# Layer 1: the norm over channels taken with the tokens still on the partitions

## The chip, the cores and the metric

The kernel runs on one core of a Trainium2 chip. Times are microseconds (us) of device time for one execution. Five engines work side by side, each through its own list of instructions in order: TensorE (PE in the profile: matmuls, and PEld for the loading of the stationary operand), VectorE (DVE), ScalarE (ACT), GpSimd (POOL) and SyncE (SP), which issues the DMA transfers. They wait for each other through semaphores. Data lies in SBUF, 128 partitions wide; matmuls write to PSUM[...], and VectorE or ScalarE must copy ("evict") results out of it. The clock that is granted to TensorE (PEclk) varies between half and full.

## The reference

A stack of four layers works on 4 images of 96 channels and 64 x 64 positions, so 16,384 tokens of 96 channels. Layer 0 is a state-space model, layer 2 linear attention and a quantised MLP, layer 3 a Fourier mixer and a second quantised MLP. The change is in layer 1, which computes, for every token:

```
h = conv7x7_depthwise(x) + conv_b
mu, var over the 96 channels
h = (h - mu) * rsqrt(var + 1e-5) * ln_g + ln_b
h = gelu(h @ w1 + b1)          # 96 -> 384, exact gelu
h = h @ w2 + b2                # 384 -> 96
x = h * layer_scale + x
```

## The kernel before

All is float32 in layer 1. `layer1` has two halves. In the first, the output of layer 0 is finished (`tokens`), put in `t` with the channels on the partitions ([96, 16384], the residual), and transposed on TensorE (`turn`) into `xt`, which has 128 neighbouring positions (two image rows) on the partitions and, in the free dimension, channel, image and row pair: `xt[128, 96, 4, 36]`. The convolution is done channel by channel as a matmul with banded 128 x 128 matrices: four matmuls per channel into one slice of a PSUM tile (four buffers) `ps[128, 4 channels, 4 images, 32 row pairs]`. A loop over 24 groups of four channels loads the bands, multiplies, and evicts the whole PSUM tile back into `xt` in one copy of 128 x 512: even groups on ScalarE (L779), odd ones on VectorE (L777). The convolution's bias isn't added there; it is carried, less its mean, in a [96, 1] vector `cb` that a small matmul makes (L740, L741).

The second half is the norm and the MLP, in 32 blocks of 512 tokens (four groups of 128). It needs the channels on the partitions. Per block:

- `back` (L786 to L791): four matmuls with the identity transpose four slices `xt[:, :, b, 2 + r + d]` to `ps[96, 512]`; the slice is the stationary operand, 96 columns that lie 4 x 36 floats, that is 576 bytes, apart. VectorE copies the result to `acc`.
- `centered` (L794 to L799): a matmul with `center` (identity minus 1/96) takes off the mean over channels; ScalarE squares the result with the bias `cb` added, VectorE copies it with `cb` added to `xc`.
- `normed` (L802 to L807): a matmul with a 96 x 96 matrix of ones sums the squares over channels, in every row; ScalarE takes Ln and then Exp of -0.5 times it (the reciprocal root), and GpSimd multiplies `xc` by it.
- `hidden` (L810 to L815): three matmuls to 384 hidden channels, each evicted by ScalarE with Gelu.
- `out` (L818 to L823): three matmuls back to 96 channels, added to the residual `t` by VectorE.

Gelu and Ln/Exp need different tables on ScalarE, so blocks go in rounds of four: all four `normed` of a round (with the `back` of the next round between them), then `hidden` and `out` of the four, with the `centered` of the next round between them. The order on TensorE, VectorE, ScalarE and GpSimd is that of the program text (`manual_schedule`): an engine that waits holds up all that is behind it. A tile's `bufs` says how many buffers it rotates through. PSUM of this half before: one bank for `tp_ps`, two for `xc_ps` and `v_ps` together, four for `g_ps`, one for `m_ps`.

Of the kernel before, what the change touches and what calls it, by code (L numbers as in the profile page):

```python
# [9 lines left out]
F32 = mybir.dt.float32  # L10
# [3 lines left out]
AF = mybir.ActivationFunctionType  # L14
ALU = mybir.AluOpType
# [3 lines left out]
B, C, HW, L = 4, 96, 64, 4096  # L19
NT = B * L  # L20
T = 1024
NSC = L // T
MB = 512
# [4 lines left out]
ACT_EXP_LN = "natural_log_exp_and_others"  # L28
# [22 lines left out]
class Net:  # L51
# [643 lines left out]
    def layer1(self, scratch, t):  # L695
        tc, nc, ins = self.tc, self.nc, self.ins
        NR = L // 128
        GC = 4
        engines = {mybir.EngineType.PE, mybir.EngineType.DVE, mybir.EngineType.Activation, mybir.EngineType.Pool}
        with ExitStack() as ctx:  # L700
            xpool = ctx.enter_context(tc.tile_pool(name="l1x", bufs=1))
            xt = xpool.tile([128, C, B, NR + 4], F32, name="xt")
            cb = xpool.tile([C, 1], F32, name="cb")
            with (
                tc.manual_schedule(engines=engines),
                tc.tile_pool(name="l1a", bufs=1) as wk,
# [28 lines left out]
                for k, chunk in enumerate(chunks):  # L735
                    if k + 1 < len(chunks):
                        tokens(*chunks[k + 1])
                    turn(*chunk)
                ps = psum.tile([128, 4, C], F32, name="cb_ps", tag="xt", bufs=4)[:C, 0, :1]
                nc.tensor.matmul(ps, self.center, self.v("c_b"), start=True, stop=True)  # L740
                nc.vector.tensor_copy(cb, ps)  # L741

                def load(g):
                    w = wk.tile([128, GC, 4, 128], F32, name="band", tag="band", bufs=3)
                    nc.sync.dma_start(w, ins["band"][g])
                    return w
# [14 lines left out]
                for g in range(C // GC):  # L761
                    if g == 8:
                        self.consts2(wk, small)
                    if g % 2 == 0 and g + 2 < C // GC:
                        x2.append(outer(g // 2 + 1))
                    w = load(g)
                    ps = psum.tile([128, GC, B, NR], F32, name="cv_ps", tag="cv", bufs=4)
                    for d in range(GC):
                        c = g * GC + d
                        for k, j in enumerate((1, 0, 2)):  # L770
                            nc.tensor.matmul(
                                ps[:, d], w[:, d, j], xt[:, c, :, 1 + j : 1 + j + NR], start=k == 0, stop=False
                            )
                        nc.tensor.matmul(ps[:, d], w[:, d, 3], x2[g // 2][:, g % 2 * GC + d], start=False, stop=True)
                    dst = xt[:, g * GC : (g + 1) * GC, :, 2 : 2 + NR]
                    if g % 2:
                        nc.vector.tensor_copy(dst, ps)  # L777
                    else:
                        nc.scalar.copy(dst, ps)  # L779

            wk = ctx.enter_context(tc.tile_pool(name="l1w", bufs=1))
            psum = ctx.enter_context(tc.tile_pool(name="l1p", bufs=1, space=PSUM))
            acc, sq, xc, g = {}, {}, {}, {}

            def back(i):
                ps = psum.tile([C, 4, 128], F32, name="tp_ps", tag="tp")  # L786
                b, r = divmod(4 * i, NR)
                for d in range(4):
                    nc.tensor.matmul(ps[:, d], xt[:, :, b, 2 + r + d], self.ident, start=True, stop=True)
                acc[i] = wk.tile([C, MB], F32, name="acc", tag="acc", bufs=5)  # L790
                nc.vector.tensor_copy(acc[i], ps.rearrange("p r n -> p (r n)"))  # L791

            def centered(i):
                ps = psum.tile([C, MB], F32, name="xc_ps", tag="ln", bufs=2)  # L794
                nc.tensor.matmul(ps, self.center, acc.pop(i), start=True, stop=True)
                sq[i] = wk.tile([C, MB], F32, name="sq", tag="sq", bufs=6)
                nc.scalar.activation(sq[i], ps, AF.Square, bias=cb)
                xc[i] = wk.tile([C, MB], F32, name="xc", tag="xc", bufs=9)
                nc.vector.tensor_scalar_add(xc[i], ps, cb)  # L799

            def normed(i):
                ps = psum.tile([C, MB], F32, name="v_ps", tag="ln", bufs=2)  # L802
                nc.tensor.matmul(ps, self.ones, sq.pop(i), start=True, stop=True)
                rs = wk.tile([C, MB], F32, name="rs", tag="rs", bufs=3)
                nc.scalar.activation(rs, ps, AF.Ln, scale=1.0 / C, bias=self.eps[:C])
                nc.scalar.activation(rs, rs, AF.Exp, scale=-0.5)  # L806
                nc.gpsimd.tensor_mul(xc[i], xc[i], rs)  # L807

            def hidden(i):
                g[i] = wk.tile([128, 3, MB], F32, name="g", tag="g", bufs=3)  # L810
                n = xc.pop(i)
                for m in range(3):
                    ps = psum.tile([128, MB], F32, name="g_ps", tag="g", bufs=4)
                    nc.tensor.matmul(ps, self.c_w1[:, m * 128 : (m + 1) * 128], n, start=True, stop=True)
                    nc.scalar.activation(g[i][:, m, :], ps, AF.Gelu, bias=self.c_b1[:, m : m + 1])  # L815

            def out(i):
                ps = psum.tile([C, MB], F32, name="m_ps", tag="m")  # L818
                for m in range(3):
                    nc.tensor.matmul(ps, self.c_w2[:, m, :], g[i][:, m, :], start=m == 0, stop=m == 2)  # L820
                g.pop(i)
                td = t[:, i * MB : (i + 1) * MB]
                nc.vector.scalar_tensor_tensor(td, ps, self.c_b2, td, ALU.add, ALU.add)  # L823


            n = NT // MB
            with tc.manual_schedule(engines=engines):
                for i in range(4):
                    back(i)
                    if i:  # L830
                        centered(i - 1)
                centered(3)
                for i in range(0, n, 4):
                    nc.scalar.preload_act_table_set(ACT_EXP_LN)
                    more = i + 4 < n
                    for d in range(4):
                        normed(i + d)
                        if more:
                            back(i + 4 + d)
                    hidden(i)  # L840
                    for d in range(4):
                        if more:
                            centered(i + 4 + d)
                        if d < 3:
                            hidden(i + d + 1)
                        out(i + d)

    def norm_steps(self, t, wk, psum):

# [499 lines left out]
def _lay_out(i):  # L1349
    f = {k: np.asarray(v) for k, v in i.items()}  # L1350
    m = {k[8:]: v for k, v in f.items() if k.startswith("L0_conv_")}
    c = {k[8:]: v for k, v in f.items() if k.startswith("L1_conv_")}
# [17 lines left out]
    for k, v in (("rd", np.diagonal(a["r"])), ("id", np.diagonal(a["i"])), ("rb", a["rb"]), ("ib", a["ib"])):  # L1370
# [22 lines left out]
        "c_w1": c["w1"],  # L1393
        "c_w2": c["w2"].reshape(3, 128, C).transpose(1, 0, 2),
        "ls_row": c["layer_scale"].reshape(1, C),
        "wkv": aug[:, C:],
        "wqt": aug[:, :C].T,
        "wff": f["L2_attn_Wff"],
# [28 lines left out]
```

## Time and profile before

The time is 4103.03 us, the median of three runs (4100.42 to 4106.08). The profiled execution spans 4106.5 us. Layer 1 in it:

| stretch | us | what it is |
|---|---|---|
| 2612 to 2676 | 64 | `tokens` and `turn` |
| 2676 to 2794 | 118 | convolution, with the loading of constants for later layers between groups 7 and 8 |
| 2794 to 3068 | 274 | norm and MLP, 32 blocks in eight rounds |

The costliest instructions of the last stretch on engines other than TensorE: Gelu 687 ns (three per block), Square 682, Ln 681 and Exp 630 on ScalarE; the copies L791 687, L799 747 and the residual add L823 747 on VectorE; the product L807 1265 on GpSimd; and 16 loads of ScalarE tables of 1283 each, two in a round.

A profile line gives start or line number, engine, operation, output<-input by the program's names, shapes and count. Durations of matmuls are modelled and overlap with those of the next ones, so their sum isn't time; the distance between starts is. A float32 matmul shows as two passes, each with its own LDWEIGHTS.

### The profile page before, as it was taken

How to read it: one execution, taken by the hardware profiler on the slowest of the kernel's cores; microseconds unless marked ns; L12 is line 12 of the kernel's file. 1: busy time of each engine (PE TensorE's matmuls, PEld its weight loads, DVE VectorE, ACT ScalarE, POOL GpSimd, SP SyncE). 2: the span in 40 equal slices, each digit the busy share in tenths (PEclk: the TensorE clock that was granted, in tenths of full speed). 3: DMA queues.
4: the chain of work that ended last, by engine and by line, in shares of the span. 5: the costliest groups of instructions: out<-in, count | busy, mean ns of one | idle time of the engine just before them, and what ended most of it. 6: DMA issues, size and time to landing. Idle time of an engine off the chain costs nothing. (4 is left out here: it accounts for less than half of the span.)

```text
span 4106.5 us, 45550 instructions
## 1 busy us (share of the span) xinstructions
PE 3374.3 (82%) x14304; PEld 1459.6 (36%) x14304; DVE 3125.3 (76%) x2382; ACT 2474.1 (60%) x4690; POOL 2988.3 (73%) x1603
## 2 busy tenths in 40 slices
PE   6788878888888888888777786779999888788987
PEld 3222222222222222222222221575446346555642
DVE  4999999999999999999999999512222673443649
ACT  4676666676667667667666664404555575544547
POOL 2999999999999999999999999321120355333528
PEclk9888878888888888888888886589999998989989
DMA  7567657566666756756656665561000000100111
GB/s 179 142 159 169 148 144 174 138 162 167 154 154 162 166 141 162 175 135 161 171 141 161 168 153 140 146 209 43 0 0 1 0 6 1 29 26 27 47 42 54
DMA packets 183146, 468.08 MB, mean 114 GB/s; under 512 B 53092, under 2 KB 55022, under 8 KB 179824
## 3 DMA queue, kind: packets, MB, share of 16 engines
q1 hardware_dynamic: 182904, 465.17, 45.6%
q8 instruction: 114, 1.87, 0.2%
q14 instruction: 128, 1.05, 0.1%
HBM read 391.48 MB, written 73.50 MB: 113 GB/s over the span
## 5 line engine op out<-in xcount | busy, mean ns | idle before, releaser
L484 POOL TENSOR_TENSOR hs<-hs,crep 128x1024 f32<-128x1024 f32 x768 | 1795.3, 2360 | 28.7 <-DVE hs L478 22.9
L442 PE MATMUL rep<-dbl,sel_b 32*128 32x512 f32 x1152 | 405.4, 780 | 465.7 <-DVE hs L478 439.4
L462 POOL TENSOR_TENSOR up<-udb,brep 128x1024 f32<-128x1024 f32 x256 | 603.9, 2359 | 7.9 <-DMA ud<-du 7.9
L456 ACT ACTIVATE da<-ddb,nega 128x1024 f32<-128x1024 f32 x512 | 584.9, 1149 | 9.7 <-DVE hs L478 8.4
L456 ACT ACTIVATE dap<-ddb,nega 128x1024 f32<-128x1024 f32 x256 | 286.2, 1118 | 418.5 <-DVE hs L478 417.0
L503 PE MATMUL y<-hs,sel_r 128*32 128x512 f32 x3072 | 475.1, 682 | 6.2 <-POOL hs L484 6.1
L478 DVE TENSOR_TENSOR_SCAN hs<-da,state,rep 128x1024 f32<-128x1024 f32 x192 | 450.8, 2348 | 16.7
L478 DVE TENSOR_TENSOR_SCAN hs<-da,state,u 128x1024 f32<-128x1024 f32 x192 | 450.9, 2348 | 10.1
L478 DVE TENSOR_TENSOR_SCAN hs<-dap,state,up 128x1024 f32<-128x1024 f32 x192 | 447.0, 2328 | 5.7 <-ACT dap L456 5.5
L442 PEld LDWEIGHTS rep<-dbl,sel_b 32*128 32x128 f32 x1152 | 108.7, 217 | 758.9 <-issue 513.7
L198 PE MATMUL ps<-n,w_x 97*64 97x512 f32 x1536 | 366.3, 620 | 4.4 <-POOL n L307 4.2
L474 DVE TENSOR_TENSOR u<-udb,rep 128x1024 f32<-128x1024 f32 x256 | 314.7, 1229 | 65.3 <-PE rep L442 43.9
L474 DVE TENSOR_TENSOR rep<-udb,rep 128x1024 f32<-128x1024 f32 x256 | 310.7, 1214 | 0.4
L1013 POOL CAST hq<-y 128x512 fp8e5<-128x512 f16 x192 | 117.9, 638 | 222.0 <-DVE y L1012 221.5
L1161 POOL TENSOR_TENSOR av<-av,ec 128x780 f32<-128x780 f32 x32 | 58.8, 1836 | 195.2 <-ACT av L1158 195.2
L198 PEld LDWEIGHTS ps<-n,w_x 97*64 97x64 f32 x1536 | 108.2, 140 | 253.4 <-issue 202.4
L503 PEld LDWEIGHTS y<-hs,sel_r 128*32 128x32 f32 x3072 | 66.4, 115 | 352.7 <-issue 190.7
L807 POOL TENSOR_TENSOR xc<-xc,rs 96x512 f32<-96x512 f32 x32 | 40.4, 1265 | 208.1 <-ACT rs L806 198.3
L370 POOL TENSOR_TENSOR du<-delta,xc 128x512 f32<-128x512 f32 x96 | 122.0, 1271 | 70.2 <-ACT delta L354 60.6
L212 PE MATMUL ps<-xc,xproj 64*102 64x512 f32 x384 | 155.1, 968 | 3.5 <-ACT xc L332 3.5
L346 ACT COPY dbl<-ps 102x512 f32<-102x512 f32 x64 | 34.3, 588 | 199.7 <-PE ps L212 199.7
L478 DVE TENSOR_TENSOR_SCAN hs<-da,rep 128x1024 f32<-128x1024 f32 x64 | 146.5, 2289 | 5.4
(261 smaller groups left out, 6673.4 us busy)
## 6 DMA issues: line engine op xcount, KB each, us to landing
ddb<-dd SPq DMA_DIRECT2D x768, 128.0 KB, 3.6
udb<-ud SPq DMA_DIRECT2D x768, 128.0 KB, 4.4
crep<-cd SPq DMA_DIRECT2D x512, 128.0 KB, 3.8
brep<-cd SPq DMA_DIRECT2D x256, 128.0 KB, 3.7
dd<-delta SPq DMA_DIRECT2D x64, 384.0 KB, 4.3
ud<-du SPq DMA_DIRECT2D x192, 128.0 KB, 2.5
band<-in_band SPq DMA_DIRECT2D x24, 1024.0 KB, 5.5
gt<-in_idft SPq DMA_DIRECT2D x64, 256.0 KB, 2.7
```

The source lines that it names most:

```text
L198: nc.tensor.matmul(ps[rows], w[:, 64 * p : 64 * p + 64], rhs[:, at.start + shift : at.stop + shift], start=k == 0, stop=k == len(ws) - 1, ...
L212: nc.tensor.matmul(ps, w[rows, p], x[rows, p], start=start and p == 0, stop=p == 2)
L370: nc.gpsimd.tensor_mul(u, m["delta"][:, of], m["xc"][:, of])
L442: nc.tensor.matmul(x[:, at], sel_b[rows, order[t][1]], made[k]["dbl"][rows, at], start=True, stop=True)
L456: nc.scalar.activation(da, made[k]["dd", h, j], AF.Exp, scale=nega[:, col : col + 1])
L462: nc.gpsimd.tensor_mul(u, made[k]["ud", h, j], made[k]["brep", g])
L474: nc.vector.tensor_mul(u, made[k]["ud", h, j], x)
L478: nc.vector.tensor_tensor_scan(hs[:, 1:], made[k].pop(("da", t)), u, 0.0 if s == 0 else st, ALU.mult, ALU.add)
L484: nc.gpsimd.tensor_mul(hs[:, :T], hs[:, 1:], made[k]["crep", order[t][1]])
L503: nc.tensor.matmul(made[k]["y", p][row : row + 32], sel_r, made[k]["hs", t][:, at], start=False, stop=True, skip_group_check=True,)
L1013: nc.gpsimd.tensor_copy(q[:, m, :], y2, saturate=False)
L1161: nc.gpsimd.tensor_add(v[:, 2:4], v[:, 0:2], ec)
```

## The change

The norm is computed before the transposition back, while the 128 partitions of `xt` are tokens and the 96 channels lie in the free dimension. Then mean and variance are sums along the free dimension, which VectorE has instructions for (BN_STATS makes partial statistics of a row, BN_AGGR mean and variance of them), and subtracting the mean and multiplying with the reciprocal root is one TENSOR_SCALAR with two values per partition. What is transposed afterwards is the normed token, in a contiguous tile `n`. The matmuls with `center` and `ones` and the product on GpSimd fall away, and Ln and Exp work on 16 values per partition for a whole round of 2048 tokens. For this the convolution's bias must be in `xt`: it is added in the evictions of the convolution, by channel, from a row that is loaded to all partitions. Statistics and roots are made two rounds ahead of their use (the first two rounds ahead of everything), the transposed blocks one round ahead. The freed PSUM banks double `tp_ps` and `m_ps`.

```diff
@@ -700,7 +700,8 @@
         with ExitStack() as ctx:
             xpool = ctx.enter_context(tc.tile_pool(name="l1x", bufs=1))
             xt = xpool.tile([128, C, B, NR + 4], F32, name="xt")
-            cb = xpool.tile([C, 1], F32, name="cb")
+            cb = xpool.tile([128, C], F32, name="cb")
+            nc.sync.dma_start(cb, ins["c_b_row"].partition_broadcast(128))
             with (
                 tc.manual_schedule(engines=engines),
                 tc.tile_pool(name="l1a", bufs=1) as wk,
@@ -736,9 +737,6 @@
                     if k + 1 < len(chunks):
                         tokens(*chunks[k + 1])
                     turn(*chunk)
-                ps = psum.tile([128, 4, C], F32, name="cb_ps", tag="xt", bufs=4)[:C, 0, :1]
-                nc.tensor.matmul(ps, self.center, self.v("c_b"), start=True, stop=True)
-                nc.vector.tensor_copy(cb, ps)
 
                 def load(g):
                     w = wk.tile([128, GC, 4, 128], F32, name="band", tag="band", bufs=3)
@@ -772,39 +770,47 @@
                                 ps[:, d], w[:, d, j], xt[:, c, :, 1 + j : 1 + j + NR], start=k == 0, stop=False
                             )
                         nc.tensor.matmul(ps[:, d], w[:, d, 3], x2[g // 2][:, g % 2 * GC + d], start=False, stop=True)
-                    dst = xt[:, g * GC : (g + 1) * GC, :, 2 : 2 + NR]
-                    if g % 2:
-                        nc.vector.tensor_copy(dst, ps)
-                    else:
-                        nc.scalar.copy(dst, ps)
+                    for d in range(GC):
+                        c = g * GC + d
+                        dst = xt[:, c, :, 2 : 2 + NR]
+                        if g % 2:
+                            nc.vector.tensor_scalar_add(dst, ps[:, d], cb[:, c : c + 1])
+                        else:
+                            nc.scalar.activation(dst, ps[:, d], AF.Identity, bias=cb[:, c : c + 1])
 
             wk = ctx.enter_context(tc.tile_pool(name="l1w", bufs=1))
             psum = ctx.enter_context(tc.tile_pool(name="l1p", bufs=1, space=PSUM))
-            acc, sq, xc, g = {}, {}, {}, {}
+            mv, rs, xc, g = {}, {}, {}, {}
+
+
+            def stats(k, d):
+                if d == 0:
+                    mv[k] = wk.tile([128, 16, 2], F32, name="mv", tag="mv", bufs=3)
+                for q in range(4 * d, 4 * d + 4):
+                    b, r = divmod(16 * k + q, NR)
+                    st = wk.tile([128, 6], F32, name="st", tag="st", bufs=4)
+                    nc.vector.bn_stats(st, xt[:, :, b, 2 + r])
+                    nc.vector.bn_aggr(mv[k][:, q], st)
+
+            def roots(k):
+                rs[k] = wk.tile([128, 16], F32, name="rs", tag="rs", bufs=3)
+                nc.scalar.activation(rs[k], mv[k][:, :, 1], AF.Ln, bias=self.eps)
+                nc.scalar.activation(rs[k], rs[k], AF.Exp, scale=-0.5)
 
             def back(i):
-                ps = psum.tile([C, 4, 128], F32, name="tp_ps", tag="tp")
-                b, r = divmod(4 * i, NR)
-                for d in range(4):
-                    nc.tensor.matmul(ps[:, d], xt[:, :, b, 2 + r + d], self.ident, start=True, stop=True)
-                acc[i] = wk.tile([C, MB], F32, name="acc", tag="acc", bufs=5)
-                nc.vector.tensor_copy(acc[i], ps.rearrange("p r n -> p (r n)"))
-
-            def centered(i):
-                ps = psum.tile([C, MB], F32, name="xc_ps", tag="ln", bufs=2)
-                nc.tensor.matmul(ps, self.center, acc.pop(i), start=True, stop=True)
-                sq[i] = wk.tile([C, MB], F32, name="sq", tag="sq", bufs=6)
-                nc.scalar.activation(sq[i], ps, AF.Square, bias=cb)
-                xc[i] = wk.tile([C, MB], F32, name="xc", tag="xc", bufs=9)
-                nc.vector.tensor_scalar_add(xc[i], ps, cb)
-
-            def normed(i):
-                ps = psum.tile([C, MB], F32, name="v_ps", tag="ln", bufs=2)
-                nc.tensor.matmul(ps, self.ones, sq.pop(i), start=True, stop=True)
-                rs = wk.tile([C, MB], F32, name="rs", tag="rs", bufs=3)
-                nc.scalar.activation(rs, ps, AF.Ln, scale=1.0 / C, bias=self.eps[:C])
-                nc.scalar.activation(rs, rs, AF.Exp, scale=-0.5)
-                nc.gpsimd.tensor_mul(xc[i], xc[i], rs)
+                k, d = divmod(i, 4)
+                n = wk.tile([128, 4, C], F32, name="n", tag="n", bufs=3)
+                for q in range(4):
+                    b, r = divmod(4 * i + q, NR)
+                    at = slice(4 * d + q, 4 * d + q + 1)
+                    nc.vector.tensor_scalar(
+                        n[:, q], xt[:, :, b, 2 + r], mv[k][:, at, 0], rs[k][:, at], ALU.subtract, ALU.mult
+                    )
+                ps = psum.tile([C, 4, 128], F32, name="tp_ps", tag="tp", bufs=2)
+                for q in range(4):
+                    nc.tensor.matmul(ps[:, q], n[:, q], self.ident, start=True, stop=True)
+                xc[i] = wk.tile([C, MB], F32, name="xc", tag="xc", bufs=7)
+                nc.vector.tensor_copy(xc[i], ps.rearrange("p r n -> p (r n)"))
 
             def hidden(i):
                 g[i] = wk.tile([128, 3, MB], F32, name="g", tag="g", bufs=3)
@@ -815,7 +821,7 @@
                     nc.scalar.activation(g[i][:, m, :], ps, AF.Gelu, bias=self.c_b1[:, m : m + 1])
 
             def out(i):
-                ps = psum.tile([C, MB], F32, name="m_ps", tag="m")
+                ps = psum.tile([C, MB], F32, name="m_ps", tag="m", bufs=2)
                 for m in range(3):
                     nc.tensor.matmul(ps, self.c_w2[:, m, :], g[i][:, m, :], start=m == 0, stop=m == 2)
                 g.pop(i)
@@ -823,27 +829,28 @@
                 nc.vector.scalar_tensor_tensor(td, ps, self.c_b2, td, ALU.add, ALU.add)
 
 
-            n = NT // MB
+            n = NT // MB // 4
             with tc.manual_schedule(engines=engines):
-                for i in range(4):
-                    back(i)
-                    if i:
-                        centered(i - 1)
-                centered(3)
-                for i in range(0, n, 4):
-                    nc.scalar.preload_act_table_set(ACT_EXP_LN)
-                    more = i + 4 < n
+                nc.scalar.preload_act_table_set(ACT_EXP_LN)
+                for k in range(2):
                     for d in range(4):
-                        normed(i + d)
-                        if more:
-                            back(i + 4 + d)
-                    hidden(i)
+                        stats(k, d)
+                    roots(k)
+                for d in range(4):
+                    back(d)
+                for k in range(n):
                     for d in range(4):
-                        if more:
-                            centered(i + 4 + d)
-                        if d < 3:
-                            hidden(i + d + 1)
-                        out(i + d)
+                        hidden(4 * k + d)
+                        if k + 1 < n:
+                            back(4 * k + 4 + d)
+                        if k + 2 < n:
+                            stats(k + 2, d)
+                        if d:
+                            out(4 * k + d - 1)
+                    if k + 2 < n:
+                        nc.scalar.preload_act_table_set(ACT_EXP_LN)
+                        roots(k + 2)
+                    out(4 * k + 3)
 
     def norm_steps(self, t, wk, psum):
 
@@ -1393,6 +1400,7 @@
         "c_w1": c["w1"],
         "c_w2": c["w2"].reshape(3, 128, C).transpose(1, 0, 2),
         "ls_row": c["layer_scale"].reshape(1, C),
+        "c_b_row": c["conv_b"].reshape(1, C),
         "wkv": aug[:, C:],
         "wqt": aug[:, :C].T,
         "wff": f["L2_attn_Wff"],
```

## The prediction

> **What bounds the kernel now.** I read the windows of the second half of layer 1 first: from the first transposition back (2794.0 us) to the first matmul of layer 2 (3067.7 us), split where the first `hidden` starts.
>
> ```profile
> core 0: us, PE busy (x) PEld busy (x) DVE busy (x) ACT busy (x) POOL busy (x), PEclk, DMA share, GB/s
> 2794.00:2814.30 20.30, 18.88 (x79) 12.77 (x80) 7.79 (x11) 9.00 (x13) 3.79 (x3) 1.00 0.01 2
> 2814.30:3067.70 253.40, 250.43 (x691) 115.65 (x689) 61.98 (x85) 140.97 (x197) 40.76 (x31) 1.00 0.00 0
> 2794.00:3067.70 273.70, 269.31 (x768) 128.41 (x768) 69.77 (x96) 149.97 (x209) 44.55 (x34) 1.00 0.00 1
> ```
>
> TensorE is busy for 269 of 273.7 us at full clock; VectorE for 70, ScalarE 150, GpSimd 45, no DMA. So this stage ends when TensorE has done its list. Next, the groups of that window (busy, mean ns; idle before them and its releaser):
>
> ```profile
> L820 PE MATMUL m_ps<-g,c_w 128*96 128x512 f32 x192 | 88.0, 594 | 1.4 <-DVE t L823 0.9
> L814 PE MATMUL g_ps<-xc,c_w 96*128 96x512 f32 x192 | 87.7, 593 | 0.6 <-ACT g L815 0.6
> ...
> L789 PE MATMUL tp_ps<-ident,xt 128*96 128x128 f32 x256 | 49.6, 336 | 1.8 <-DVE xt L777 0.9 <-DVE acc L791 0.8
> ...
> L803 PE MATMUL v_ps<-sq,ones 96*96 96x512 f32 x64 | 32.8, 597 | 0.7 <-DVE xc L799 0.5
> L795 PE MATMUL xc_ps<-acc,center 96*96 96x512 f32 x64 | 32.7, 593 | 0.0
> ```
>
> Each f32 matmul is two passes. Busy means overlap, so the price of a pass is the distance between starts, read in the timeline (start, length):
>
> ```profile
> 2908.96 1.58 PE L789 MATMUL tp_ps<-ident,xt 128*96 128x128 f32 x8
> ...
> 2910.38 1.02 PE L803 MATMUL v_ps<-sq,ones 96*96 96x512 f32 x2
> ...
> 2910.58 0.69 DVE L791 COPY acc<-tp_ps 96x512 f32<-96x512 f32 x1 [1.68 <-PE tp_ps L789]
> 2911.32 1.39 PEld L789 LDWEIGHTS tp_ps<-ident,xt 128*96 128x96 f32 x8 [0.77 <-DVE acc L791]
> ```
>
> Eight transposing passes take 2910.38 - 2908.96 = 1.42 us (0.178 each); one slot of `normed` and `back` takes 2911.32 - 2908.96 = 2.36 us, since the next transposition waits for the eviction of the one PSUM buffer. Six passes of `hidden` or `out` take 2.57 us (0.43 each: in this timeline L814 starts at 2881.57, L795 after it at 2884.14). A round of four blocks is 4 x 2.36 + 4 x (2.57 + 2.57 + 0.86) = 33.4 us, and eight are 267 of the 273.7.
>
> **What the skill says.** (1) "Vector Engine (DVE) Microarchitecture Reference", section 5.2: a port keeps its rate only in runs of two adjacent words; one source hopping at every element costs 1.73 ns a column instead of 1.05. The trace agrees for a write: L729 below steps 576 bytes at each element, and 801 ns less about 154 fixed is 1.69 ns an element, where L777, without a step, has (692 - 154)/512 = 1.05. (2) "ScalarE: Activation LUTs", What ACT_TABLE_LOAD costs: a pointer operand adds about 93 ns to an ACTIVATE; here a 512-wide copy takes 593 ns (L779) and an Identity with a bias 677 (L534). (3) "TensorE: Matmul & The Clock Gate", What's actually happening: after an idle window of 3.4 us the array runs at half clock until a busy one. In the trace of before TensorE resumes dense work at 2602.4 and has full clock again at about 2605.6. No page prices the statistics instruction.
>
> **The change, part by part.** *Off TensorE:* per block `centered` (0.86) and `normed` (0.86) go, and so does the 0.77 wait between transpositions, with two PSUM buffers. The transpositions stay, but their stationary operand is now `n`, contiguous. The nearest group is L1213 of layer 3, contiguous and of the same 128*96 128x128 shape:
>
> ```profile
> 3786.86 1.04 PE L1213 MATMUL m_ps<-gt,bt 128*96 128x128 f32 x8
> ```
>
> Its last pass is 0.27 long, so the distance is (1.04 - 0.27)/7 = 0.11 us, and eight take 0.89; the other end is today's 1.42. I take 0.89, as the shape and layout are the same. A block then costs TensorE 2.57 + 0.89 + 2.57 = 6.03 us, a round 24.1.
>
> *Onto VectorE:* per 128 tokens one BN_STATS over 96 elements 576 bytes apart, a BN_AGGR and a TENSOR_SCALAR with two pointer scalars; off it the 747 ns of L799. Rows to price them by:
>
> ```profile
> L729 DVE COPY xt<-xt_ps 128x384 f32<-128x384 f32 x16 | 12.8, 801 | 24.2 <-PE xt_ps L725 24.2
> L777 DVE COPY xt<-cv_ps 128x512 f32<-128x512 f32 x12 | 8.3, 692 | 86.1 <-PE cv_ps L774 86.1
> ...
> L155 DVE TENSOR_SCALAR aug<-ident,vec 96x96 f32<-96x96 f32 x2 | 0.5, 263 | 0.0
> ...
> L596 DVE TENSOR_REDUCE mv<-sums 96x1 f32<-96x32 f32 x1 | 0.2, 182 | 7.2 <-ACT x L534 7.2
> ```
>
> A reduction has 182 - 32 x 1.04 = 149 ns fixed; 96 strided elements make 149 + 96 x 1.7 = 0.31 us (0.25 if the stride is free, 0.39 at the 2.5 ns that the same table of the skill has for its worst step). BN_AGGR on six values is like a tiny op, 0.16 (up to 0.25). With gaps, a dependent pair takes 0.50 (0.40 to 0.68), so S = 2.0 us of statistics per block (1.6 to 2.7). TENSOR_SCALAR: 0.26 as in L155, plus something for stride and second pointer, 0.27 in sequence: T = 1.1 per block (0.8 to 1.6). Copy 0.73 and residual add 0.79 with gaps stay. VectorE has 2.0 + 1.1 + 0.73 + 0.79 = 4.6 us of work in a slot of 6.03.
>
> *Do they hide?* In a slot VectorE must do, after the transpositions end: start 0.2, copy 0.73, statistics 2.0, residual add 0.75, four scalings 1.1, 0.2 to the last transposition: 5.0, while TensorE does `out` and `hidden` and transposes (6.03): hidden. At the top costs it is 6.2 to 6.3, a few tenths over. Only slot 0 of a round has no `out` between transpositions: TensorE has 2.57 + 0.89 = 3.46 there, VectorE 0.93 + 2.0 + 1.1 + 0.2 = 4.24. That wait of 0.8 us (0 to 2.0) holds up `out` and everything behind it, in the six rounds that take statistics.
>
> *ScalarE:* three Gelus of 0.69 a block; Ln and Exp shrink to 16 columns a round, with the same two table loads of 1.28. They wait for the last statistics of the round, about 3 us after its last transposition; Ln, Exp (0.6) and a table load give 4.9, and the next round's first Gelu is wanted at 2.57 x 2 + 0.43 + 0.2 = 5.8, behind two `out`. At no cost. GpSimd falls idle at no cost.
>
> *New head:* nothing of the round may start before 32 statistics pairs: 32 x 0.50 = 16.0 us (12.8 to 21.8), then four backs of 1.1 + 0.4 + 0.73, less the last copy, 8.0 (6.8 to 10.0). `hidden` starts 24.0 us after the convolution, against 20.3 now. TensorE idles through 16 of it, so its clock halves; one busy window at half clock, 3.4 us, loses about 2 (1.6 to 3.4).
>
> *Convolution evictions:* four of 128 columns with a bias in place of one of 512: on VectorE about 4 x 0.35, on ScalarE 4 x 0.37, every 7 us, both idle over 6 us before each such eviction; hidden by TensorE's matmuls with four PSUM buffers. The last one ends the stage 0.3 earlier or 0.7 later. The removed bias matmul (0.4) lies beside the last copy; the bias load costs one issue of at most 0.4 on the DMA queue ahead of `o`. Together +0.4.
>
> **The sum.** After the convolution: 24.0 + 6 x (24.1 + 0.8) + 24.1 (no statistics) + 8 x 2.57 (no backs) + 1.0 (last add until layer 2) = 219.1, against 273.7; plus 2 for the clock and 0.4: -52. 4103 - 52 = **4051 us**.
>
> **Rivals.** *A, VectorE becomes the bound (18%).* If a statistics pair takes 0.9 and a scaling 0.45 (dependent small ops waiting on each other), S = 3.6, T = 1.8: a round is VectorE's sum 4 x (3.6 + 1.8 + 1.52 + 0.4) = 29.3, the head 28.8 + 11 = 40. 40 + 6 x 29.3 + 26 + 20.6 + 1 = 263: 4095 at that end, 4075 halfway. For it: twelve small serial ops a block, none like them in the trace. Against: dependent small ops of VectorE start 0.19 apart (L598 to L600). *B, the saving is larger (12%):* bottom costs give 19.6 + 6 x 24.1 + 24.1 + 20.6 + 1 + 2 = 212, 4041. *C, slower (4%):* the clock stays halved after the idle head, as it does for 72 us under the narrow transpositions of the first half of the layer (windows of 2640 to 2676: clock 0.50, TensorE busy throughout). The list of about 190 us would double to 380: 4240. Against: that stage has 96-column passes, this one 512-column ones, and layer 0 leaves half clock within one window under those. Also slower would be small VectorE ops above 1.6 us per 128 tokens; nothing points there. *D, no difference (2%):* costs at A's far end and beyond, about 4103.
>
> **How the numbers follow.** Forecast 64%, A 18, B 12, C 4, D 2. The predicted time is the forecast's. The top costs of all terms give 31.8 + 6 x (25.0 + 2.0) + 25 + 20.6 + 1 + 3.4 = 244, 4073; the bottom ones 4041, less some for the shorter tail with two `m_ps` buffers. Range 4036 to 4075, which leaves out the upper half of A, C and D. Faster by over 0.2%: 0.93; within: 0.02; slower: 0.05.
>
> **What would show it.** Right: in the rounds TensorE is idle only in a short wait for `n` once a round, and transposing passes start 0.11 us apart; BN_STATS near 0.31 us; a head of 24 us at half clock. Wrong: transpositions waiting for VectorE in every slot (A), half clock through the stage (C), or Gelus waiting for a table load.

## The result, and the profile after

The changed kernel takes **4060.6 us** (median of four runs, 4057.2 to 4066.6) against 4103.0 before (four runs, 4100.4 to 4106.1): a ratio of 0.9892, 95% interval 0.9878 to 0.9905. That is 42 us less; the forecast was 4051, 52 less, in a range of 4036 to 4075.

The same view as in the prediction, the windows of the second half, now from the last matmul of the convolution (2798.7) to the first of layer 2, split at the first `hidden` (columns: PE, PEld, DVE, ACT and POOL busy, clock, DMA share, GB/s):

```profile
2798.70:2825.40 26.70, 8.08 (x36) 6.93 (x35) 19.94 (x87) 7.46 (x9) 0.00 (x0) 0.60 0.00 0
2825.40:3020.40 195.00, 192.65 (x610) 92.10 (x609) 111.92 (x365) 85.79 (x121) 4.32 (x2) 0.99 0.00 1
2798.70:3020.40 221.70, 200.74 (x644) 99.03 (x642) 131.86 (x452) 93.25 (x130) 4.32 (x2) 0.95 0.00 1
```

Behind the head TensorE is busy for 192.7 of 195.0 us: it still sets the end, with a shorter list. VectorE has gone from 70 to 132 us and doesn't. The groups of that window:

```profile
L820 PE MATMUL g_ps<-xc,c_w 96*128 96x512 f32 x192 | 88.8, 599 | 0.0
L826 PE MATMUL m_ps<-g,c_w 128*96 128x512 f32 x192 | 86.3, 592 | 0.0
...
L811 PE MATMUL tp_ps<-ident,n 128*96 128x128 f32 x256 | 37.9, 296 | 20.1 <-DVE n L806 20.1
L792 DVE BATCH_NORM_STATS2 st<-xt 128x6 f32<-128x96 f32 x128 | 37.4, 292 | 0.1
L806 DVE TENSOR_SCALAR n<-xt,mv,rs 128x96 f32<-128x96 f32 x128 | 37.1, 350 | 0.0
...
L793 DVE BATCH_NORM_AGGREGATE mv<-st 128x2 f32<-128x6 f32 x128 | 23.3, 182 | 4.4
```

`center`, `ones` and the product on GpSimd are gone. TensorE's wait is for `n`: 20.1 us, 15.3 of them one wait in the head. Slots 0 and 1 of a round on TensorE in the timeline (start, length):

```profile
2851.33 2.74 PE L820 MATMUL g_ps<-xc,c_w 96*128 96x512 f32 x6
2853.90 1.04 PE L811 MATMUL tp_ps<-ident,n 128*96 128x128 f32 x8
2854.78 2.74 PE L820 MATMUL g_ps<-xc,c_w 96*128 96x512 f32 x6
2857.77 1.18 PE L811 MATMUL tp_ps<-ident,n 128*96 128x128 f32 x8 [0.25 <-DVE n L806]
2858.79 2.74 PE L826 MATMUL m_ps<-g,c_w 128*96 128x512 f32 x6
```

Eight transposing passes take 2854.78 - 2853.90 = 0.88 us, as forecast (0.89). In the slot without an `out` the transposition should start 2.57 after 2854.78, at 2857.35; it starts at 2857.77, 0.42 late, for `n`. A round is 24.66 us (the L820 at 2851.33 returns at 2875.99).

Where the 42 us came from, by stage (us, one profiled execution each). The second column is the changed kernel run again, beside later experiments:

| stage | before | after | after, again |
|---|---|---|---|
| end of layer 0's statistics to first use of an `o` | 4.6 | 6.9 | 6.2 |
| to the first convolution matmul | 58.6 | 58.5 | 58.6 |
| convolution to the second w1raw cast (L646) | 51.3 | 55.9 | 53.7 |
| to the last convolution matmul | 65.0 | 66.2 | 64.9 |
| second half, to layer 2 | 274.9 | 221.7 | 222.0 |
| layer 2 | 302.6 | 306.9 | 306.2 |

The second half gained 53.2, where the forecast had 52.6 (219.1 and 2 for the clock against 273.7). The first half lost 8.0 (3.9 in the second execution) and layer 2 lost 4, which the forecast had at 0.4 and nothing. Layer 3, behind this table, takes 728 to 744 us in these executions without order. Effects of a few us are therefore read from stages here, and not from total times.

### The profile page after: what moved, and what is told of

Its sections match the earlier page's. It is cut to its first block, busy times and chain, and to the rows that moved or that the text cites. A ratio compares the mean times of both kernels' runs of the same rounds, so it can differ in the third digit from the quotient of the medians.

```text
span 4058.1 us, 45524 instructions
## 1 busy us (share of the span) xinstructions
PE 3311.3 (82%) x14174; PEld 1427.9 (35%) x14174; DVE 3193.0 (79%) x2769; ACT 2424.3 (60%) x4647; POOL 2948.0 (73%) x1571
## 5 line engine op out<-in xcount | busy, mean ns | idle before, releaser
L503 PEld LDWEIGHTS y<-hs,sel_r 128*32 128x32 f32 x3072 | 66.2, 116 | 359.2 <-issue 192.2
```

What stands on the lines that cost most here:

```text
L503: nc.tensor.matmul(made[k]["y", p][row : row + 32], sel_r, made[k]["hs", t][:, at], start=False, stop=True, skip_group_check=True,)
```

## The experiments

The theory: TensorE's list bounds the second half, the loss in the first half belongs to the convolution's bias, and the one in layer 2 to the clock. The rivals: VectorE, or the waits for PSUM, bound the second half.

**1. The bias alone.** The kernel before, with the row of the bias loaded and added in the evictions; the old norm without `cb`.

```diff
+            nc.sync.dma_start(cb, ins["c_b_row"].partition_broadcast(128))
...
-                        nc.vector.tensor_copy(dst, ps)
...
+                            nc.vector.tensor_scalar_add(dst, ps[:, d], cb[:, c : c + 1])
...
-                nc.scalar.activation(sq[i], ps, AF.Square, bias=cb)
+                nc.scalar.activation(sq[i], ps, AF.Square)
...
-                nc.vector.tensor_scalar_add(xc[i], ps, cb)
+                nc.vector.tensor_copy(xc[i], ps)
```

> The kernel before with one part of the change alone: the bias row loaded to all partitions and added per channel in the convolution's evictions; the norm as before, without the bias in its evictions. Theory 1 (my prediction: the first half of the layer pays about 0.4 us, and the 8 us by which this half was longer in the changed kernel's trace, 2.3 before the first load lands, 4.6 until the second set of weights lands and 1.2 after, come from how transfers happened to land): 4103 within 3. Theory 2 (the bias load and the shorter evictions cost these 8 us): 4110 to 4112, with the first load 6 to 7 us after the end of layer 0's statistics in place of 4.6, and the convolution 122 us long in place of 116.

Measured: 4113.4 against 4107.9 for the kernel before on that chip, 1.0013 (1.0004 to 1.0022): slower by some 5 us. The first use of `o` comes after 6.8 us, the second w1raw cast after 55.0; the second half has 275.1, as before. So the loss of the first half is the bias's, and not the new loop's: this kernel has the old one.

**2. A second PSUM buffer alone.** The kernel before with two `tp_ps` (and three `g_ps`).

```diff
-                ps = psum.tile([C, 4, 128], F32, name="tp_ps", tag="tp")
+                ps = psum.tile([C, 4, 128], F32, name="tp_ps", tag="tp", bufs=2)
...
-                    ps = psum.tile([128, MB], F32, name="g_ps", tag="g", bufs=4)
+                    ps = psum.tile([128, MB], F32, name="g_ps", tag="g", bufs=3)
```

> The kernel before with two PSUM buffers for the transposition back (three in place of four for the hidden layer). Theory 1 (TensorE's own passes are the time; the wait for the one buffer showed on the weight loads, 0.77 us each, but the distance between slots was 2.36 against 1.42 + 0.86 = 2.28 of passes, so only 0.08 us a block is lost): second half of layer 1 272 us in place of 275. Rival (the wait of 0.77 us a block is real and most of the gain is the second buffer): 252 us.

Measured: 4101.6 (one run, 4107.9 before); second half 269.2 us. The timeline of this kernel:

```profile
2903.10 1.43 PE L789 MATMUL tp_ps<-ident,xt 128*96 128x128 f32 x8
2904.37 1.02 PE L803 MATMUL v_ps<-sq,ones 96*96 96x512 f32 x2
2905.23 1.43 PE L789 MATMUL tp_ps<-ident,xt 128*96 128x128 f32 x8
```

A slot is 2.13 us, in place of 2.36, which over 28 slots makes 6.4; 5.7 were gained, twice what was expected and far from the rival's 23. The second `tp_ps` is a tenth of the change's gain; the second `m_ps` wasn't tried alone. The 0.77 us that L789 showed as idle before was almost all beside other work: it stands on a weight load (PEld), which runs ahead of the matmul.

**3. The new loop without the bias.** The changed kernel with the evictions of before; the addition of the convolution's bias is left out.

```diff
-            nc.sync.dma_start(cb, ins["c_b_row"].partition_broadcast(128))
...
-                            nc.vector.tensor_scalar_add(dst, ps[:, d], cb[:, c : c + 1])
...
+                        nc.vector.tensor_copy(dst, ps)
```

> The changed kernel without the bias row's load and with the convolution's evictions as before, one copy of 512 columns per group (leaves out the addition of the convolution's bias). Theory 1 (bias part is free): 4060 within 3. Theory 2 (it costs the 8 us of the first half): 4052 to 4053. Both: second half of layer 1 still about 221 us.

Measured: 4060.5, 0.9881 (0.9863 to 0.9899). By the total that is what was expected if the bias part is free, and not the 4052 to 4053 expected if it costs 8 us. The stages speak for the cost: first `o` after 4.4 us and w1raw cast after 51.0, the values of before; second half 221.4. But the rest of the convolution took 66.9, so that it lasts 118.0 in all, little under the 118.6 of the changed kernel's second execution. So the two places of the loss are the bias's; that the whole kernel is faster without it isn't shown.

**4. The row loaded later.** The changed kernel, the bias row issued behind the first two chunks of `tokens`.

```diff
-            nc.sync.dma_start(cb, ins["c_b_row"].partition_broadcast(128))
...
                 tokens(*chunks[0])
+                tokens(*chunks[1])
+                nc.sync.dma_start(cb, ins["c_b_row"].partition_broadcast(128))
...
-                    if k + 1 < len(chunks):
+                    if 1 < k + 1 < len(chunks):
```

> The changed kernel with the bias row's load issued behind the loads of the first two chunks in place of ahead of them. Theory 2a (the load of 128 short rows ahead of the first chunk delays that by 2.3 us): first load used 4.6 us after layer 0's statistics in place of 6.9, time 4058. Theory 1 (the 2.3 us is chance of landing): 4060, and the distance scatters between 4.5 and 7 whatever the order.

Measured: 4060.1, 0.9880 (0.9863 to 0.9897), a total that doesn't tell the two expectations apart; first `o` after 4.4 us. With the row in front it is 6.0 to 6.9 in every kernel. A load of 48 KB that is issued 0.4 us ahead of `o` delays it by some 2: the prediction counted the issue, not the transfer. The w1raw cast stays late (54.7).

**5. Two buffers for the raw weights.** The rest of the first half's loss lies between groups 7 and 8, where constants of later layers are prepared. The DMA queue there, of the kernel before:

```profile
2713.17 2.67 SPq L745 DMA_DIRECT2D band<-in_band  x1
2715.93 0.88 SPq L644 DMA_DIRECT2D w1raw<-in_f_w  x1
```

and of the changed one:

```profile
2715.63 1.95 SPq L743 DMA_DIRECT2D band<-in_band  x2
2724.71 0.33 SPq L644 DMA_DIRECT2D w1raw<-in_f_w  x1
```

The second `w1raw` has one buffer and waits for the cast of the first (at 2712.6 before, 2713.8 after). SyncE isn't among the engines ordered by hand; in the changed kernel's list the load stands behind two loads of bands instead of one, and the second band waits in turn for a buffer. So it is in all nine kernels with the bias in the evictions and one buffer for `w1raw`; in the three without that bias it is one band. TensorE waits at L685 for what hangs on it, 26.0 us against 22.1. Experiment:

```diff
-            a = wk.tile([C, HID], F32, name="w1raw", tag="raww1")
+            a = wk.tile([C, HID], F32, name="w1raw", tag="raww1", bufs=2)
...
-            a = wk.tile([128, 3, C], F32, name="w2raw", tag="raww2")
+            a = wk.tile([128, 3, C], F32, name="w2raw", tag="raww2", bufs=2)
```

> The changed kernel with two buffers for the raw weights of the two quantised layers (w1raw, w2raw) in the constants between convolution groups 7 and 8. Theory (the 4 us that the convolution lost come from the load of the second w1raw: it waits for its one buffer, which the longer evictions free 1.2 us later, and the schedule then puts it behind two band loads instead of one, so that it is issued 8.8 us later): with two buffers its place no longer matters, the wait of 17.6 us on VectorE and of 26 us on TensorE shrinks to under 10 (bn_rows and a_w2raw must still come), the convolution takes about 108 in place of 122 us, time 4046. Rival (the longer evictions themselves slow the convolution): still 118 or more, time 4057 to 4060.

Measured: 4056.8, 0.9870 (0.9853 to 0.9886), so the total is the rival's, and isn't told from the changed kernel's 4057.7 and 4060.6; the convolution takes 112.8 us instead of 122.1 (118.6 in the second execution, 116.3 before). The chain of waits has a new last member:

```profile
PE w_ps L685 <- DVE bn_d L681: 18.5, 1, 18.5
ACT bn_s L664 <- DMA bn_rows<-in_bn_rows: 17.0, 1, 17.0
```

The wait for `w1raw` is gone; the one for `bn_rows`, loaded behind it, takes its place (17.0 on ScalarE, 18.5 on TensorE), so of the fall to 108 that was expected about two thirds came.

**6. TensorE kept busy in the head.** Unread matmuls (17, then one behind each of the four first backs) while the first statistics run.

```diff
...
+                warm(17)
                 for k in range(2):
...
                 for d in range(4):
                     back(d)
+                    warm(1)
```

> The changed kernel with matmuls of no use (the centering matrix times the first block of t, result never read) filling TensorE while the statistics of the first two rounds are made. Theory (5 of the 27 us from the convolution's end to the first hidden matmul are the halved clock: transposing passes 0.21 in place of 0.11 us and the first three hidden passes 0.85 in place of 0.43): that stretch 22 to 23 us, and full clock throughout. If the half clock at the start of layer 2 (4 to 5 us there) is tied to the clock's restart in this head, layer 2 takes 302 in place of 307 us; if it is tied to what TensorE does at the seam, 307. Rival (the statistics and their chain alone set the head): 26 to 27 us.

Measured: 4060.0 (one run). The clock is full throughout; the head takes 25.0 us instead of 26.7, and from the first `hidden` to the last `out` 192.3 instead of 193.5. These 2.9 us are what is left when the filling itself is paid: the first transposition comes 1.22 us behind the first scaling instead of 0.48, as it stands behind the 17, and the first `hidden` waits for a last unread matmul of 0.86. The later backs come 2.32 to 2.41 us apart instead of 3.13 to 3.16. So the halved clock costs some 4.5 us (an estimate: 2.9 + 0.74 + 0.86), near the 5 expected here, and not the 2 of the prediction. Layer 2 takes 306.1: its halved clock isn't tied to that of the head.

**7. Even slots.** Statistics run five blocks ahead, a transposition one ahead, and the roots come where a round's statistics end; the prologue has one round of statistics and one back.

```diff
...
+                for i in range(4):
+                    ahead(i)
+                back(0)
+                ahead(4)
+                for i in range(n):
+                    hidden(i)
+                    if i + 1 < n:
+                        back(i + 1)
+                    ahead(i + 5)
+                    if i:
+                        out(i - 1)
...
```

> The changed kernel with its loop made even: each slot has one hidden, one back (one block ahead), one out and the statistics of the block five ahead, and the roots come in the third slot of a round; before the first slot only one round of statistics. Theory (TensorE's 6.03 us a slot is the bound wherever VectorE's 1.7 of statistics and 1.15 of scaling have an out beside them; the head and the slots without an out are what is left): head 12 to 13 in place of 27 us, 32 slots 193 us without the half-microsecond waits, second half of layer 1 about 206 in place of 221, time 4046 to 4049. Rival (VectorE bounds the slots once no slack is given): slots of 6.4 us and more, second half 217 or more.

Measured: 4046.9, 0.9845 (0.9831 to 0.9860). The head takes 15.1 us instead of 26.7; the second half 211.5. Behind the head TensorE waits for `n` no more, so the rival, VectorE as the bound, falls; the 196.4 us there aren't less than the 195.0 of the changed kernel, because three transpositions have moved into them (2.6 us), the clock is still half for their first 4.7 (2.6 in the changed kernel), and TensorE waits twice for `xc` (1.6 in all). The expectation was 206; part of the difference is that in the short head Ln and Exp each wait for a table load of 1.28 us, and VectorE 3.3 us for the two. The Trainium skill ("ScalarE: Activation LUTs", section What ACT_TABLE_LOAD costs) puts the load at about 1283 ns and a whole switch, with a drain, at about 2.66 us. The trace agrees with the load and shows no more than it: Exp starts 1.30 us after its load does. It shows two of these loads between the last statistics and the first scaling, although a preload stood in the text.

**8. The normed tile with a step.** `n` is laid out `[128, 96, 4]`, so a transposition's stationary operand has its columns 16 bytes apart.

```diff
-                n = wk.tile([128, 4, C], F32, name="n", tag="n", bufs=3)
+                n = wk.tile([128, C, 4], F32, name="n", tag="n", bufs=3)
...
```

> The changed kernel with the normed tile n laid out as 96 x 4, so that a stationary operand's columns lie 16 bytes apart in place of adjacent. Theory (the fall from 0.178 to 0.11 us per transposing pass is the contiguous stationary operand): passes 0.175 apart, 0.5 us more a block, second half of layer 1 about 236 us in place of 221. Rival (it is something else, as the order of loads): passes stay 0.11, 221 us; the scalings may get a little longer either way.

Measured: 4083.4 (one run); the timeline of this kernel:

```profile
2864.87 1.50 PE L811 MATMUL tp_ps<-ident,n 128*96 128x128 f32 x8
2866.21 2.74 PE L826 MATMUL m_ps<-g,c_w 128*96 128x512 f32 x6
```

Eight passes take 1.34 us instead of 0.88, and 28 times the 0.46 makes 12.9 of the 13.0 us by which the second half is longer. Shown: contiguity is what makes the transposition cheap. The step doesn't have to be the 576 bytes of `xt`; 16 are enough.

**9. Statistics twice.** Each BATCH_NORM_STATS2 is issued a second time into an unread tile.

```diff
                     nc.vector.bn_stats(st, xt[:, :, b, 2 + r])
+                    st2 = wk.tile([128, 6], F32, name="st2", tag="st2", bufs=2)
+                    nc.vector.bn_stats(st2, xt[:, :, b, 2 + r])
```

> Every BATCH_NORM_STATS2 is issued twice (the second result is unread): 128 more of 0.29 us, 37 us of VectorE. TensorE-bound theory: a slot holds 3.5 us of VectorE beside 6.03 us of passes and would hold 4.7, so only the head (32 of the 128 stand before the first hidden pass, +9.3 us) and the round's last slot are longer (up to +1.2 us in six rounds): second half +10 to +17 us. VectorE-bound theory (rival): all 37 us show.

Measured: 4058.2, against 4057.7 for the changed kernel beside it; second half 226.9 us against 222.0. Both expectations had the price of the addition wrong. The timeline of this kernel (L794 is the second issue):

```profile
2801.44 0.29 DVE L792 BATCH_NORM_STATS2 st<-xt 128x6 f32<-128x96 f32 x1
2801.64 0.30 DVE L794 BATCH_NORM_STATS2 st<-xt 128x6 f32<-128x96 f32 x1
2801.86 0.16 DVE L795 BATCH_NORM_AGGREGATE mv<-st 128x2 f32<-128x6 f32 x1
2801.94 0.28 DVE L792 BATCH_NORM_STATS2 st<-xt 128x6 f32<-128x96 f32 x1
```

The distance from one token group to the next goes from 0.42 to 0.50 us: most of the addition lies in the time for which the aggregate waited for its statistics anyway. It puts 128 x 0.084 = 10.8 us on VectorE, 2.7 of it in the head. The head is longer by 2.7, the rounds by 2.2. Six slots 0 have 6 x 4 x 0.084 = 2.0 us of it; the 6.0 in the other 18 slots don't show. That is TensorE-bound with one tight slot a round; a bound VectorE would show all 10.8.

**10. The tail filled.** Unread transposing passes of the identity in the last four slots, for the theory that layer 2's slow start follows from a long stretch of wide passes alone.

```diff
                         if k + 1 < n:
                             back(4 * k + 4 + d)
+                        else:
+                            ps = psum.tile([C, 4, 128], F32, name="fill_ps", tag="tp", bufs=2)
+                            for q in range(4):
+                                nc.tensor.matmul(ps[:, q], self.ident[:, :C], self.ident, start=True, stop=True)
```

> Four unread transposing passes of the identity in each of the last four slots, where the changed kernel has only 512-column passes. Streak theory: the half clock at the start of layer 2 follows from more than 20 us of wide passes without a short one; with the short ones in place layer 2's start takes about 302 us (from 306) and the second half grows by 4 x 0.43 = 1.7 us: 2 to 3 us faster than the changed kernel. Rival: the fill changes nothing there (306 to 307 us) and the kernel is about 2 us slower.

Measured: 4065.3, against 4057.7 for the changed kernel beside it; the second half is 3.3 us longer (four times the 0.88 of eight passes, not the 0.43 counted above), and layer 2 takes 306.8. The streak theory falls.

**11, 12. Three edits together, and the changed kernel again.** The even slots of 7, the late row of 4 and the buffers of 5; beside it the changed kernel as it is.

> Three edits on the changed kernel at once: the even slots, the bias row loaded behind the first two chunks, and two buffers for the raw weights. If the parts are independent, each removes its own stretch: first load again about 4.4 us behind the statistics of layer 0 (from 6.1), convolution about 113 us (from 118 to 122), second half about 211 us, start of layer 2 about 302 us; from 4046.9 for the even slots alone that is 4046.9 - 2 - 6 = about 4039. Rival: the shorter convolution only moves the wait to the next constant (as the wait for bn_rows did), and the time stays within 3 us of the even slots alone, 4044 to 4047.

> The changed kernel, unaltered, on the same chip as the others of this set: 4058 to 4062 if the chip is like the earlier ones; second half about 221 us, start of layer 2 about 306 us.

Measured: **4033.9** (four runs, 4030.8 to 4041.7), 0.9829 of before (0.9815 to 0.9844), for the three together; 4057.7, 0.9888 (0.9873 to 0.9903), for the changed kernel. By stage against that one: first `o` 4.6 us (6.2), convolution 112.4 (118.6), second half 211.8 (222.0), layer 2 299.8 (306.2), together -24.4, with 23.8 between the medians. (The two profiled executions are only 11.7 apart: layer 3 took 10.0 us longer in the one with the edits.) The first three are independent, as expected; the last, 6.4 us, is the next point. This version beats both kernels.

## Layer 2's first microseconds

In the changed kernel the clock halves just behind the seam to layer 2. The Trainium skill ("TensorE: Matmul & The Clock Gate", section What's actually happening) says that activity is judged over a window of 3413 ns that runs freely, whatever the program does. The trace agrees in its lengths: the stretches of half clock here are 17.07, 23.89 and 27.31 us, which are 5, 7 and 8 times 3.413. So the edges of these stretches tell where the windows lie. Two windows at the seam, of the changed kernel run again:

```profile
3016.18:3019.59 3.41, 1.83 (x5) 0.65 (x5) 0.75 (x1) 0.59 (x1) 3.33 (x1) 1.00 0.00 0
3019.59:3023.00 3.41, 2.73 (x4) 0.66 (x3) 0.69 (x1) 1.91 (x3) 3.41 (x2) 0.50 0.00 0
```

and of the one with statistics twice:

```profile
3021.75:3025.16 3.41, 2.57 (x6) 0.73 (x5) 1.05 (x2) 0.00 (x0) 1.26 (x1) 1.00 0.00 0
3025.16:3028.58 3.42, 2.58 (x6) 0.57 (x4) 0.00 (x0) 1.48 (x3) 3.42 (x2) 1.00 0.00 0
```

(The length comes first, then how long TensorE was busy; the last column but two is the clock.) The two have the same instructions in the last two rounds and behind them, and the same waits of 0.84 and 0.74 us before the first two matmuls of layer 2. In the first kernel both waits lie in one window, TensorE is busy for 1.83 of its 3.41 us, and the clock halves at its end. In the second an edge parts the waits; the clock stays, and layer 2 is done in 301.6 us. So the cause isn't the work at the seam alone. For all kernels, with the point in its window at which the first matmul of layer 2 starts, and the least time that TensorE was busy in one window at the seam:

| kernels | point in the window, us | least busy, us | layer 2, us |
|---|---|---|---|
| changed loop, eight executions | 0.78 to 1.31 | 1.55 to 1.89, then half clock | 306.1 to 307.8 |
| changed loop, statistics twice | 2.93 | 1.96 | 301.6 |
| even slots (7, 11) | 0.57, 0.30 | 2.10, 2.35 | 301.7, 299.8 |
| old loop (before, 1, 2) | 2.23, 2.91, 3.29 | 1.96, 1.96, 2.24 | 302.6, 300.5, 301.1 |

The eight that halve lie together, and they alone have a window with less than 1.9 us of work. The prediction took from the same page that the clock halves after an idle window; here a window in which TensorE works for about half of the time is enough. It is a match over fourteen executions, not a test that moved the seam alone. Nor is the busy time the whole rule: elsewhere in the changed kernel run again a window with 1.52 us of work (at 1824.93) keeps the full clock, and one with 2.06 (at 2357.41) loses it. Whether the executions that were timed without a profile fell alike isn't known.

## Why the prediction was right, and where it was off

- **What bounds the stage**: right. TensorE's list sets the second half: 221.7 us from the last convolution matmul, 220.1 from the first statistics, where the prediction's count begins, against 219.1 + 2. Experiment 9 tells it from a bound on VectorE, experiment 2 from the PSUM wait.
- **Off TensorE**: right. A block takes 6.03 us where nothing waits, and the price of a contiguous transposition, taken from L1213, holds (0.88); experiment 8 shows that the layout is its reason. The remark that the 0.77 wait falls away was wrong as a gain (experiment 2), but the sum used the whole slot of 2.36 and wasn't touched.
- **Onto VectorE**: statistics 0.29 us (forecast 0.31), aggregate 0.18 (0.16), a pair 0.42 (0.50), four scalings 1.14 to 1.18 (1.1). The pair came out low, since the next statistics start 0.10 behind an aggregate.
- **Slot 0's wait**: right in place, 0.42 instead of 0.8, which follows from the pair. A round is 24.66 (24.9); the transposition that waits is also stretched, 1.02 us instead of 0.88, as its four scalings arrive one by one.
- **The head**: 25.1 us from the first statistics (24.0, and 2 for the clock in all). The statistics take 13.5 (16.0), and the four backs, from the first transposition on, 11.2 (8.0): the prediction counted one busy window at half clock, but the four transpositions, with over 1 us between them, ran at half clock too, 0.8 us dearer each than at full clock in experiment 6. In all the halved clock costs some 4.5 us, not 2. (In the kernel before the clock is full from 2604.7, not about 2605.6 as the prediction read it.) That cheaper statistics and dearer backs nearly cancel is luck.
- **ScalarE**: right in the rounds. Its Gelus wait for no roots. The Trainium skill ("ScalarE: Activation LUTs", section What ACT_TABLE_LOAD costs) has a pointer operand at about 93 ns: the Squares of experiment 1, without their bias, take 592 ns and before 682, which agrees.
- **The convolution's evictions and the load of the row**: the term of the sum that was most too small. The prediction put it as "the bias load costs one issue of at most 0.4 on the DMA queue ahead of `o`. Together +0.4", and gave no price to the transfer, nor to the loads of other layers' constants in the same queue. The evictions themselves cost no more than was said (four of 343 ns on VectorE in 1.13 us, four of 370 on ScalarE in 1.14) and are hidden. But the row's transfer delays the first `o` by about 2 us (experiments 3 and 4: shown), and a weight load slid behind a second load of bands (experiments 1, 3 and 5: that it is the bias and that it is this buffer are shown; that 0.4 us of longer evictions tipped the order of the list is inferred). In the profile of the result the first half lost 8.0 us, in the seven other kernels with the same first half 3.8 to 7.5.
- **Not foreseen**: 4 us at the start of layer 2.

In the two profiled executions the sum is then -53.2 + 8.0 + 4.3 = -41. That it lies so close to the -42 of the medians is partly luck: these two executions are 48.4 apart, as layers 0 and 3, which the change doesn't touch, were 7.5 shorter in the second. With the changed kernel's other execution the sum is -52.9 + 3.9 + 3.6 = -45, and its median lies 47.0 below that of the kernel before beside it. The forecast's -52 had the first number right and missed the two others, outside the stage it was looking at.

## What to carry to other kernels

Do the statistics of a norm where the normed dimension is the free one: VectorE had room beside a TensorE-bound loop, and two matmuls a block were saved, with a faster transposition because its operand became contiguous. Price a new load by what it delays, and look at the list of every queue whose order isn't written by hand: a single-buffered load next to the edit cost its stage more than the edit's own instructions, though the total time doesn't resolve it. A prologue that fills a pipeline two rounds deep is paid in full; one round of statistics and one back were enough (experiment 7). With that and two small changes to loads the kernel gained another 24 us, 6 of them at the start of layer 2, which seem to follow the windows of the clock and can't be counted on.

## What the runs showed of the hardware

- Two BATCH_NORM_STATS2 that don't depend on each other start 0.20 us apart, though each is recorded with 0.29; an aggregate of the one just issued starts 0.32 behind it. Putting another group's statistics between would hide about 0.12 a pair, some 3.8 us of the changed kernel's head of 32 pairs (an estimate from these distances; not tried).
- A float32 transposition whose stationary columns lie 16 bytes apart takes 0.168 us a pass, at 576 bytes 0.16 to 0.18, contiguous 0.11.
- The clock stayed halved for 17.07 us at the start of layer 2, where TensorE was busy for 75 to 100% of the time (in stretches of 5 us). The same instructions ran at full clock where an edge of the 3.413 us windows fell between their waits.
